# Random-feature attention: the third norm step of a chunk one slot earlier in a hand-written order

## The chip, the cores and the metric

The kernel runs on one core of one Trainium2 chip. The time is device microseconds of one execution of the whole program, from the first to the last instruction and the little around them. The program has sixteen layers in a row; the change lies in one of them.

## What is computed

The activation x has 4096 tokens of 128 channels (a batch of 16 by 256 tokens). The program adds sixteen sublayers to it in turn, each on a layer norm of x. The third one is a Performer block: attention with 16 heads of 8 channels by way of 32 random features, and a feed-forward behind it. The attention part of the reference, cut:

```python
def _phi(u, omega):
    proj = jnp.einsum('bhsk,mk->bhsm', u, omega)
    sq = 0.5 * jnp.sum(u * u, axis=-1, keepdims=True)
    stab = jnp.max(proj, axis=-1, keepdims=True)
    return jnp.exp(proj - sq - stab) / jnp.sqrt(m) + 1e-06
...
q = jnp.einsum('bsd,dhk->bhsk', x, wq)
...
pq = _phi(q * scale, omega)
pk = _phi(k * scale, omega)
kv = jnp.einsum('bhsm,bhsk->bhmk', pk, v)
z = jnp.sum(pk, axis=2)
num = jnp.einsum('bhsm,bhmk->bhsk', pq, kv)
den = jnp.einsum('bhsm,bhm->bhs', pq, z)
out = num / den[..., None]
```

The x that goes in here is the layer norm `(x - mean) / sqrt(var + 1e-5)` of the running x, without a gain. That norm is what the change touches.

## The kernel before, in words

Channels lie on the 128 partitions, tokens along the free axis. `self.x` is the running activation, `self.ha` its norm (both 128 x 4096), `self.hb` the attention's result. The work is cut in 8 chunks of 512 tokens (`CH`, `NCH`), 16 batch entries of 256 (`B`), and 32 tiles of 128 (`NTILE`). One batch entry is half a chunk.

`performer_attend` (line 2275) writes its order out by hand. Its list `steps` (2401 to 2406) has entries (slot, every, many, what). `tiles_in_slots` (2260) runs a counter k, here from -7 to 45. In each k it walks down the list, and where `(k - slot)` is a multiple of `every`, it calls `what` with the quotient. [...] So the list's order is the order within one k, and one chunk's work recurs every four k.

The steps that matter here, for chunk c with batch entries 2c and 2c + 1:

- `norm(0)`, `norm(1)`, `norm(2)` (2400): the three parts of the norm of x (`norm_x_step`, 1837; `norm_steps`, 1817). The first, `centre_step` (1759), is a matmul of x with the centring matrix, a copy from PSUM to `ha` on ACT, and a square `nsq` on POOL. The second, `spread_step` (1774), is a matmul of the square with a matrix of means, and a logarithm and an exponential on ACT that leave 1/sqrt(var) in `nrs`. The third, `scale` (1828), is one multiply on DVE, `ha <- ha * nrs` (128 x 512, by way of line 531).
- `project` (2287): two matmuls of `ha` with wq and wk (in the trace four records ps<-ha,w, as each fp32 matmul has two), copied on ACT to q and k (both named `q`), and squared on POOL.
- `values` (2306): four matmuls with `ha` as the stationary side (ps<-w,ha).
- `lengths` (2297): eight matmuls with 16 columns (ps<-w,sq), and on DVE a copy to `nrm` (2304).
- `features` (2315), per batch entry: sixteen small matmuls into four PSUM banks (ps<-w,q), and on DVE four maxima (2331), two small additions and four subtractions (f<-ps,sub).
- `raised` (2341): two exponentials on ACT, and a multiply-add on POOL (2345).
- `turn` (2363): four transposes of `f` (ps<-ct,f), copied on ACT to `ft`.
- `sums` (2347): eight matmuls with 33 columns (ps<-v,f), two multiplies on DVE to `kv`.
- `heads` (2372): matmuls ps<-ft,kv at 2377, `rd` on ACT, `ot` on DVE.
- `out` (2385): ps<-ot,w, and an addition on DVE into `hb`. `end(0)` to `end(2)` (2391): the norm of that result, with the same three parts, in place in `hb`.

PSUM has eight banks: four for the features (tag `f`), four for all else (tag `ps`), shared out by `share` (2407). Which of the four a matmul gets is decided when the program is built, by the place of the instructions that free them.

`norm_x_step` does nothing for a chunk whose norm the stage before has already made (`self.led`, 1839): `lead` (1862) does so for chunks 0 to NCH - 4 = 4. In this stage, then, the three norm steps run for chunks 5, 6 and 7 alone.

Of the kernel before, what the change touches and what calls it, by code (L numbers as in the profile page):

```python
# [21 lines left out]
NCH = NT // CH  # L22
# [469 lines left out]
class Net:  # L492
# [70 lines left out]
    def norm(self, src, dst, eps, g=None, b=None, rms=False, chunks=range(NCH)):  # L563

        nc = self.nc
        with ExitStack() as st:
            pool = self.pool(st, "norm", 2)
            pv = self.bank()
            last = len(chunks) - 1
            for n, c in enumerate(chunks):  # L570
                s, d = src[:, self.chunk(c)], dst[:, self.chunk(c)]
                sq = pool.tile([P, CH], F32, tag="sq", name="sq")
                if rms:
                    self.gt(sq, s, s, ALU.mult)
                else:
                    pc = self.bank()
                    self.mm(pc, self.k["cent"], s)
                    self.act(d, pc, AF.Copy)
                    self.gt(sq, d, d, ALU.mult)
                self.mm(pv[:8], self.k["vrow"][:, 7 - c : 15 - c], sq, start=n == 0, stop=n == last)  # L580
            rs = pool.tile([8, CH], F32, tag="rs", name="rs", bufs=1)
            self.act(rs, pv[:8], AF.Sqrt, bias=self.k[eps][:8])
            nc.vector.reciprocal(rs, rs)
            for c in chunks:
                s = src[:, self.chunk(c)] if rms else dst[:, self.chunk(c)]
                d = dst[:, self.chunk(c)]
                pb = self.bank()
                self.mm(pb, self.sel[:, c, :], rs)
                if g is None:
                    self.tt(d, s, pb, ALU.mult)  # L590
                else:
                    self.stt(d, s, g, pb, ALU.mult, ALU.mult)
                    if b is not None:
                        self.act(d, d, AF.Identity, bias=b)
# [1055 lines left out]
class Fast(Net):  # L1650
# [624 lines left out]
    def performer_attend(self, w):  # L2275
# [6 lines left out]
        with ExitStack() as st:  # L2282
# [108 lines left out]
            def end(i):  # L2391
# [8 lines left out]
            norm = lambda i: lambda c: self.norm_x_step(p, c, i)  # L2400
# [1 line left out]
                (13, 4, NCH, end(2)), (12, 4, NCH, end(1)), (11, 4, NCH, end(0)), (10, 4, NCH, out),  # L2402
                (7, 2, B, heads), (5, 2, B, sums), (3, 1, NTILE, turn), (1, 2, B, raised), (0, 2, B, features),
                (-1, 4, NCH, lengths), (-2, 4, NCH, values), (-3, 4, NCH, project),
                (-4, 4, NCH, norm(2)), (-6, 4, NCH, norm(1)), (-7, 4, NCH, norm(0)),
            ]
            with self.share(f=4, ps=4):
                self.tiles_in_slots(-7, NTILE + 14, steps)
# [1467 lines left out]
```

## Time and profile before

| | us |
|---|---|
| median of 3 runs (lowest, highest) | 4220.33 (4219.34, 4223.46) |
| profiled execution | 4218.15 |
| its span, first to last instruction | 4216.4 |
| attention part of the Performer block, about | 820 to 1015 |
| in it: TensorE busy | 170.78 of 195.00 |
| in it: DVE, ACT, POOL busy | 125.71, 97.47, 65.31 |

The profile is of one execution, on a machine of five engines: TensorE (PE, its weight loads PEld), VectorE (DVE), ScalarE (ACT), GpSimd (POOL) and SyncE (SP, which issues transfers). A row of a timeline has the start in us from the span's start, a length, the engine, the line in the kernel, the operation, what it writes and reads, a count where equal ones are merged, and in brackets how long the engine stood idle before it and whose end released it. Lines 504, 508, 528, 531, 534 and 543 are helpers that many steps call; the names of the tiles tell which step an instruction belongs to. The clock that is named with a stretch is the share of TensorE's full clock that was granted there.

### The profile page before, as it was taken

The numbers are of one execution on the slowest core, as the hardware profiler recorded it, in microseconds if no ns is written. First come the engines' busy times: TensorE is split into PE (matmuls) and PEld (weight loads), VectorE is DVE, ScalarE is ACT, GpSimd is POOL, SyncE is SP. The second block draws the span as 40 slices with busy tenths as digits, with TensorE's granted clock in tenths as the row PEclk, the third lists the DMA queues.
The fourth block names the chain that finished last, engine by engine and source line by source line (L and its number), as shares of the span: only waits on it lengthen the run. The fifth ranks groups of instructions, "written<-read, shape, count | busy, mean of one in ns | idle before, by whom it ended". The sixth has DMA issues, their size and how long they took to land. (4 is left out here: it accounts for less than half of the span.)

```text
span 4216.4 us, 74153 instructions
## 1 busy us (share of the span) xinstructions
PE 3831.5 (91%) x29030; PEld 2182.7 (52%) x29030; DVE 2551.0 (61%) x4503; ACT 2281.8 (54%) x4478; POOL 1853.7 (44%) x1632
## 2 busy tenths in 40 slices
PE   7999999998899999985989869888999999899978
PEld 3555466464455466454965459543444344455333
DVE  4776576374577477473346633556877676486474
ACT  6665466555766466652457634444554454774532
POOL 4754365232565166225433434454555455321251
PEclk8999999998999999996999979999999999999979
DMA  1800000000000000004920058100000000000000
GB/s 61 347 15 12 11 9 9 22 1 1 20 11 14 6 7 9 6 11 142 323 69 12 17 182 295 41 19 21 16 14 16 8 0 10 7 2 19 6 0 21
DMA packets 110086, 190.88 MB, mean 45 GB/s; under 512 B 16126, under 2 KB 70788, under 8 KB 109600
## 3 DMA queue, kind: packets, MB, share of 16 engines
q1 hardware_dynamic: 97248, 162.83, 11.7%
q0 software_dynamic: 9120, 18.51, 1.3%
q8 instruction: 231, 3.78, 0.4%
q10 hardware_dynamic: 3360, 4.72, 0.3%
q14 instruction: 127, 1.04, 0.1%
HBM read 118.28 MB, written 54.20 MB: 41 GB/s over the span
## 5 line engine op out<-in xcount | busy, mean ns | idle before, releaser
L528 ACT ACTIVATE pt<-ps 128x512 f32<-128x512 f32 x640 | 339.5, 600 | 337.5 <-PE ps L504 336.2
L504 PE MATMUL ps<-hb,w 128*128 128x512 f32 (+1 forms) x960 | 463.7, 617 | 3.9 <-issue 3.3
L504 PE MATMUL ps<-w,hb 128*128 128x512 f32 (+2 forms) x896 | 405.2, 573 | 27.3 <-DVE t L531 18.5
L534 POOL TENSOR_TENSOR t<-t,t 128x512 f32<-128x512 f32 x256 | 319.9, 1271 | 153.7 <-DVE t L531 107.8
L531 DVE TENSOR_TENSOR t<-ps,tab 128x512 f32<-128x512 f32 x512 | 317.5, 681 | 70.1 <-ACT sq L528 66.7
L534 POOL TENSOR_TENSOR t<-t,ss 128x1024 f32<-128x1024 f32 x128 | 243.7, 1904 | 195.2 <-ACT ss L528 194.0
L504 PEld LDWEIGHTS ps<-hb,w 128*128 128x128 f32 (+1 forms) x960 | 179.6, 191 | 261.8 <-issue 220.6
L528 ACT ACTIVATE qkt<-ps 128x512 f32<-128x512 f32 x256 | 140.6, 595 | 299.2 <-PE ps L508 299.2
L531 DVE TENSOR_TENSOR u<-u,ps 128x384 f32<-128x384 f32 (+1 forms) x206 | 121.8, 595 | 277.2 <-ACT u L528 114.9
L534 POOL TENSOR_TENSOR nsq<-ha 128x512 f32<-128x512 f32 x112 | 123.2, 1100 | 354.3 <-ACT ha L528 342.3
L531 DVE TENSOR_TENSOR ot<-ps,rd 128x512 f32<-128x512 f32 (+2 forms) x224 | 143.2, 639 | 209.8 <-ACT rd L528 209.8
L504 PEld LDWEIGHTS ps<-w,hb 128*128 128x128 f32 x896 | 154.1, 193 | 174.4 <-issue 111.7
L534 POOL TENSOR_TENSOR both<-pt 128x1024 f32<-128x1024 f32 x64 | 151.2, 2363 | 199.0 <-DVE pt L531 191.3
L504 PE MATMUL ps<-ot,w 128*128 128x512 f32 x448 | 213.6, 611 | 17.4 <-DVE ot L531 9.9
L504 PE MATMUL ps<-xt,w 128*128 128x128 f32 x1704 | 221.0, 280 | 1.6 <-ACT xt L528 1.5
L2225 POOL DMA_INDIRECT back<-y,x x142 | 139.1, 980 | 186.1 <-ACT y L528 69.5
L504 PE MATMUL ps<-u,w 128*128 128x512 f32 (+1 forms) x448 | 215.4, 605 | 3.4 <-POOL u L534 3.4
L504 PEld LDWEIGHTS ps<-xt,w 128*128 128x128 f32 x1704 | 204.5, 194 | 3.4 <-ACT xt L528 3.4
L528 ACT ACTIVATE u<-ps,w 128x512 f32<-128x512 f32 x160 | 107.7, 685 | 173.3 <-PE ps L504 170.6
L3479 PE MATMUL ps<-qkt 64*128 64x192 f32 (+1 forms) x2048 | 181.8, 311 | 9.6 <-ACT rd L528 9.6
L504 PE MATMUL ps<-ha,w 128*128 128x512 f32 x320 | 176.1, 672 | 11.6 <-ACT f L528 10.2
L504 PE MATMUL ps<-nsq,ct 128*128 128x512 f32 x272 | 154.5, 652 | 30.8 <-POOL nsq L534 26.6
(366 smaller groups left out, 8756.2 us busy)
## 6 DMA issues: line engine op xcount, KB each, us to landing
w<-in_moe_x SPq DMA_DIRECT2D x142, 533.0 KB
rows<-t SPq DMA_DIRECT2D x64, 520.0 KB
nrs<-nrow SPq DMA_DIRECT2D x220, 64.0 KB
x<-rows SPq DMA_DIRECT2D x142, 65.0 KB
w<-in_local_f SPq DMA_DIRECT2D x8, 659.5 KB
y<-back ACTq DMA_DIRECT2D x16, 256.0 KB
y<-back SPq DMA_DIRECT2D x16, 256.0 KB
w<-in_local_f SPq DMA_DIRECT2D x4, 658.5 KB
```

Of the source, the lines that this page charges most:

```text
L504: self.nc.tensor.matmul(out, lhsT, rhs, start=start, stop=stop)
L528: self.nc.scalar.activation(out, in_, func, **kw)
L531: self.nc.vector.tensor_tensor(out, a, b, op)
L534: self.nc.gpsimd.tensor_tensor(out, a, b, op)
L2225: nc.gpsimd.indirect_dma_start(views[i], bass.IndirectOffsetOnAxis(ap=x[:, C : C + 1].bitcast(I32), axis=0), y, None, bounds_check=2 * NT ...
L3479: nc.tensor.matmul(out, kt[rows, g, t * P : t * P + P], qt[rows, g, t * P : t * P + wide], start=(i, t) == (0, 0), stop=i == 1, skip_group ...
```

## The change

One number in the list of slots: `norm(2)` of chunk c runs at k = 4c - 5 in place of 4c - 4.

```diff
                 (-1, 4, NCH, lengths), (-2, 4, NCH, values), (-3, 4, NCH, project),
-                (-4, 4, NCH, norm(2)), (-6, 4, NCH, norm(1)), (-7, 4, NCH, norm(0)),
+                (-5, 4, NCH, norm(2)), (-6, 4, NCH, norm(1)), (-7, 4, NCH, norm(0)),
```

The slot 4c - 4 is even and holds `features` of a batch entry; the norm's entry stands behind it in the list. The slot 4c - 5 is odd and holds no features; in it the entry stands behind `end(0)`, `heads`, `sums`, `turn`, `raised` and `lengths`. On DVE the multiply `ha <- ha * nrs` of chunks 5, 6 and 7 thereby moves from the place behind the four subtractions of `features` to the place in front of its first maximum, right behind the copy of `nrm`. In the built program these three instructions are all that changes place, on any engine. Two things follow from it there: the projection waits for the multiply at its new place; and the banks of tag `ps` are dealt out otherwise from chunk 5 on. The centring matmul of the next chunk's `norm(0)`, which took the bank that `heads` had used and waited for `ot` on DVE, takes the bank of the first projection and waits for its copy q on ACT; the output matmul takes the bank of `heads`.

## The prediction

> **What bounds the kernel now.** Three views, in this order: the busy times of the page, to know which engine counts; the stretches of the stage, one for each group of four slots; and the timeline of two such groups side by side. TensorE is busy 91% of the span, so what it loses by standing still is what the stage can give.
>
> ```profile
> PE 3831.5 (91%) x29030; PEld 2182.7 (52%) x29030; DVE 2551.0 (61%) x4503; ACT 2281.8 (54%) x4478; POOL 1853.7 (44%) x1632
> ...
> 883.54:904.72 21.18, 19.07 (x184) 13.07 (x184) 15.46 (x31) 13.06 (x21) 8.49 (x9) 1.00 0.00 1
> 904.72:931.35 26.63, 23.24 (x184) 15.10 (x184) 16.77 (x32) 13.28 (x21) 8.72 (x9) 0.81 0.00 1
> 931.35:958.31 26.96, 23.57 (x185) 15.30 (x184) 16.77 (x32) 13.28 (x21) 8.70 (x9) 0.81 0.00 1
> 958.31:982.01 23.70, 20.31 (x180) 14.25 (x180) 16.05 (x32) 11.48 (x18) 7.67 (x8) 0.86 0.00 1
> ```
>
> The last four lines are stretches (start:end, length; busy time and count of PE, PEld, DVE, ACT, POOL; granted clock; DMA). Each starts where a group of four slots begins, with the transposes in front of a chunk's projection: chunks 4, 5, 6 and 7. Chunk 4's norm was made in the stage before (chunks up to NCH - 4 = 4 are led), those of 5, 6 and 7 are made here. Chunk 4's group has the 184 matmuls of chunk 5's, takes 21.18 us against 26.63, at a granted clock of 1.00 against 0.81. It is a specimen of the group without the multiply of `norm(2)` behind the features; the timeline shows what the difference consists of (start, length, engine, line, operation; in brackets the idle time before it and who ended it).
>
> ```profile
> 883.54 0.63 PE L508 MATMUL ps<-ct,f 128*128 128x128 f32 x4
> 884.01 1.98 PE L504 MATMUL ps<-ha,w 128*128 128x512 f32 x4
> 888.09 1.13 PE L504 MATMUL ps<-x,ct 128*128 128x512 f32 x2 [2.11 <-ACT q L528]
> 889.05 1.02 PE L504 MATMUL ps<-ot,w 128*128 128x512 f32 x2
> 890.44 1.17 PE L504 MATMUL ps<-w,q 32*128 32x128 f32 x32
> ...
> 899.46 2.17 POOL L2345 TENSOR_SCALAR f<-f 128x1024 f32<-128x1024 f32 x2 [2.90 <-ACT f L528]
> 899.52 0.29 DVE L2304 COPY nrm<-ps 128x128 f32<-128x128 f32 x1 [0.87 <-PE ps L504]
> 902.00 1.29 DVE L2331 TENSOR_REDUCE sub<-ps 128x16 f32<-128x512 f32 x2 [2.18 <-PE ps L504]
> 904.72 0.63 PE L508 MATMUL ps<-ct,f 128*128 128x128 f32 x4
> 906.36 1.29 DVE L531 TENSOR_TENSOR f<-ps,sub 128x512 f32<-128x512 f32 x2
> 907.57 1.03 DVE L531 TENSOR_TENSOR ha<-ha,nrs 128x512 f32<-128x512 f32 x1
> 907.68 1.06 ACT L528 ACTIVATE f<-f 128x1024 f32<-128x1024 f32 x1 [0.75 <-DVE f L531]
> 908.74 3.75 PE L504 MATMUL ps<-ha,w 128*128 128x512 f32 x4 [3.39 <-ACT f L528]
> ```
>
> Chunk 4's projection (ha,w) follows its transposes at once. Chunk 5's waits 3.39 us. The profile names ACT's exponential, which ended last (908.74); but the matmul reads `ha`, and the multiply that makes `ha` ended at 908.60, behind all of the features' work on DVE. So the wait that ends last here is the multiply's. Then the four projection matmuls take 3.75 us, not 1.98: TensorE runs at half clock. Looked at in pieces of 0.2 us the clock is 0.50 from 907.3 to 914.1, from 934.5 to 941.5 and from 961.9 to 965.3, each time out of such a gap.
>
> **The change, part by part.** Three DVE instructions move (chunks 5, 6, 7), nothing is added or removed; SP, POOL, ACT and PE keep their order. None of the three issues a DMA. At chunk 5 the multiply leaves its place behind the features (907.57) for the place behind the copy of `nrm` (899.81).
>
> Does it fit there? Its input `nrs` was finished by ACT at 894.95 (894.32 plus 0.63), and the square that reads the old `ha` on POOL at 891.95. DVE is idle from 899.81 to 902.00, when the features' matmuls end: 2.18 us of cover for a multiply of 1.03 us. It ends at about 900.84 and is free; without that cover it would hold up the first reduction by 1.03 us, three times. [...] The row of 1.03 us was taken beside a POOL operation; where POOL is still, the same multiply takes 0.68 (at 823.08). The new place is beside two POOL operations on `f`, 899.46 to 901.63. [...] By the row the multiply ends at 900.84. [...] What POOL loses to it is hidden, since the transposes that read these values come a slot or more later.
>
> **What is late next.** With `ha` there at 901 the projection starts behind its transposes, near 905.2. The next matmul is the centring of the following chunk (x,ct). In the changed program it takes the PSUM bank of the first projection, as it does at chunk 4, and so waits for ACT's copy q, which stands behind both exponentials; at chunk 4 that is the gap of 2.11 us. ACT's second exponential stays where it is (its features on DVE are not moved), so chunk 5 copies chunk 4: x,ct starts 4.55 us after the transposes start (888.09 - 883.54). The output matmul needs `ot`, which DVE has 1.03 us earlier than before.
>
> From the start of the transposes to the start of the next features' matmuls (w,q):
> - chunk 4: 890.44 - 883.54 = 6.90 us;
> - chunk 5: 915.45 - 904.72 = 10.73, saved 3.83;
> - chunk 6: 942.42 - 931.35 = 11.07, saved 4.17;
> - chunk 7: 966.99 - 958.31 = 8.68. No norm follows, so only `ot` gates the output. At chunk 4 `ot` ends 1.89 us after DVE leaves the features' last subtraction (886.38 to 888.27); here it leaves it at 961.16, so `ot` ends at 963.05, the output starts at some 963.15, and w,q 1.39 later, at 964.54: saved 2.45.
>
> Sum 10.45 us, of which the gaps give about 10.2 less what the waits for q and `ot` take back, and the lost half clock the rest.
>
> **The second slow window.** Chunks 5, 6 and 7 also lose 1.6 us each later in the group: from w,q to the group's end chunk 5 takes 15.90 us, chunk 6 15.89, chunk 4 14.28; chunk 7 15.02 against 13.42 (14.28 less the 0.86 of one spreading it hasn't). There the clock is 0.50 for one window of 3.4 us, and TensorE was not idle in front:
>
> ```profile
> 922.00:924.00 2.00, 2.00 (x20) 2.00 (x20) 1.66 (x5) 1.16 (x2) 0.00 (x0) 1.00 0.00 0
> 924.00:926.00 2.00, 2.00 (x7) 1.05 (x7) 0.29 (x1) 1.33 (x2) 1.45 (x2) 0.59 0.00 0
> 926.00:928.00 2.00, 2.00 (x21) 1.48 (x23) 0.00 (x0) 1.53 (x3) 0.64 (x1) 0.56 0.00 0
> ```
>
> [...] By the row, 4 us of narrow matmuls (33 and 16 columns, 920.36 to 924.3) are enough, where a counter window falls inside them. All drops here lie whole multiples of about 3.41 us apart. Such a stretch drops the clock in three groups of this stage and leaves it alone in three; chunk 5's, moved to 916.5 to 920.5, would leave 0.4 us of wide matmuls in the window that ends at 920.9, and with 0.36 us (948.3 to 951.7) the clock fell. So I count one of three windows gone, 1.61 us, and keep none and all for the range.
>
> **The sum.** 10.45 + 1.61 = 12.06 us off the profiled execution's 4218.15: 4206.1. The median of the runs shown is 2.18 higher, a shift that I keep: 4208.3. What follows the stage starts earlier by the same amount; the stage's only weight load lies in its first 20 us, so no transfer pins its end.
>
> **The rivals.**
> - Forecast, 0.78: 4208.3; own range 4203.5 (all three windows gone: 15.3 off the median is 4205.0, less 1.5 of scatter) to 4211.5 (none gone 4209.9, and the port rule's 0.9).
> - The clock doesn't follow, 0.09: the shorter gap of 2.1 us, with transposes and narrow matmuls in front, still halves it. For: narrow work alone did so at 924. Against: chunk 4 has just this sequence at 1.00. Price: one window of 1.61 in each group, 10.45 - 4.83 = 5.6 saved: 4214.7.
> - The multiply is not hidden, 0.06: POOL or the copy of `nrm` holds it, and the features start its 1.03 us later, three times: 10.45 - 3.09 = 7.4 saved, 4213.0. Against: the idle 2.18 us.
> - The gap was ACT's, 0.04: the projection really waits for the exponential that the profile names. Then nothing is saved, 4220.3. Against: chunk 4's projection ran 2.5 us before its exponential began.
> - Slower, 0.03: DVE works in order, so a multiply that waits for a late `nrs` holds the whole of the features behind it, then both exponentials, q, and the next centring. Place: between `nrm` and the first reduction. Price: each us that `nrs` comes after 900.97 (902.00 - 1.03). The saving of 3.48 us a group is eaten once `nrs` comes at 904.5; one slot later still, at 907.5, would give 4220.3 + 9 = 4229. Against: 894.95 in the row is 9.5 us ahead of that point.
>
> **How the numbers follow.** Two tenths of a per cent is about what a measurement of this kernel can tell from no change: 8.4 us. Faster by more needs 4211.9 or less: nearly all of the forecast and some of the third case, 0.76. Slower is the last rival, 0.03; the rest is 0.21. The range goes from the forecast's low end, 4203.5, up to 4214.5, and leaves the clock's rival at its edge and the two last ones out.
>
> **What would show it.** In the changed profile: no idle time in front of ha,w at chunks 5 to 7; about 2.1 us in front of x,ct, ended by q; ha,w at 2.0 us for its four; the multiply between the copy of `nrm` and the reduction, whose idle time shrinks from 2.18 to about 1.1; groups of 21.2 to 22.8 us, near clock 1.00. It is wrong if ha,w still waits, if the reductions start late, or if the clock stays near 0.81.

## The result, and the profile after

The changed kernel takes 4214.95 us (median of 20 runs, 4202.33 to 4222.73) against 4221.45 us for the kernel before, timed on the same chip (20 runs, 4217.73 to 4229.9). The ratio is 0.9978, with a 95% interval from 0.997 to 0.9985: some 9 us less. (It is taken over all runs of both; the two medians lie 6.5 us apart, the two means 8.7.) The two kernels were paired twice more, on two chips: 0.9976 (0.9967 to 0.9986), 10.1 us, and 0.9974 (0.9965 to 0.9983), 10.9 us. The change makes the kernel faster by about a quarter of a per cent, near ten microseconds. The profiled execution, the fastest of the twenty, took 4202.33 us and its span 4200.5.

First the busy times of the page, then the stretches of the stage as they were shown of before (start:end, length; busy time and count of PE, PEld, DVE, ACT, POOL; granted clock; DMA): the groups of chunks 4, 5, 6 and 7.

```profile
PE 3809.4 (91%) x29030; PEld 2173.6 (52%) x29030; DVE 2554.9 (61%) x4503; ACT 2284.6 (54%) x4478; POOL 1853.7 (44%) x1632
...
884.53:905.91 21.38, 19.33 (x184) 12.99 (x184) 17.59 (x31) 13.08 (x21) 8.69 (x9) 1.00 0.00 1
905.91:927.03 21.12, 19.07 (x184) 13.08 (x184) 16.76 (x32) 13.08 (x21) 8.86 (x9) 1.00 0.00 1
927.03:948.16 21.13, 19.08 (x184) 13.08 (x184) 16.77 (x32) 13.08 (x21) 8.87 (x9) 1.00 0.01 2
948.16:971.14 22.98, 20.55 (x180) 14.27 (x180) 14.74 (x31) 11.28 (x18) 7.55 (x8) 0.85 0.00 1
```

Chunks 5 and 6 have become what chunk 4 was: 21.12 and 21.13 us at a clock of 1.00, where they took 26.63 and 26.96 at 0.81. Chunk 7 gained little, 23.70 to 22.98, and its clock is still 0.85. TensorE's busy time fell by 22.1 us over the span with the same 29030 matmuls: a matmul at half clock is counted busy for about twice as long (four of the projection 3.75 us for 1.98), so most of such a fall is clock and not work. Only 8.4 us of it lies in these three groups (67.12 to 58.70); the rest is clock elsewhere in this one execution, and no effect of the change is shown there. The timeline of one group shows how it comes about (start, length, engine, line, operation; in brackets the idle time and who ended it).

```profile
900.65 2.49 POOL L2345 TENSOR_SCALAR f<-f 128x1024 f32<-128x1024 f32 x2 [2.90 <-ACT f L528]
900.72 0.29 DVE L2304 COPY nrm<-ps 128x128 f32<-128x128 f32 x1 [0.87 <-PE ps L504]
900.93 1.31 DVE L531 TENSOR_TENSOR ha<-ha,nrs 128x512 f32<-128x512 f32 x1
902.00 1.17 PE L504 MATMUL ps<-w,q 32*128 32x128 f32 x32
903.19 1.29 DVE L2331 TENSOR_REDUCE sub<-ps 128x16 f32<-128x512 f32 x2 [0.95 <-PE ps L504]
905.91 0.63 PE L508 MATMUL ps<-ct,f 128*128 128x128 f32 x4
```

The multiply now stands at 900.93 and ends at 902.24; DVE then still waits 0.95 us for the features' matmuls. Their first maximum starts 1.19 us after the matmuls themselves (902.00 to 903.19), 2.54 us after POOL's first operation, exactly as before (899.46 to 902.00): the multiply cost nothing. The same stretch on TensorE alone:

```profile
905.91 0.63 PE L508 MATMUL ps<-ct,f 128*128 128x128 f32 x4
906.38 1.98 PE L504 MATMUL ps<-ha,w 128*128 128x512 f32 x4
910.40 1.13 PE L504 MATMUL ps<-x,ct 128*128 128x512 f32 x2 [2.04 <-ACT q L528]
911.37 1.02 PE L504 MATMUL ps<-ot,w 128*128 128x512 f32 x2
912.23 0.60 PE L508 MATMUL ps<-ct,f 128*128 128x128 f32 x4
912.76 1.17 PE L504 MATMUL ps<-w,q 32*128 32x128 f32 x32
```

The projection has no idle time in front of it any more. The idle 3.39 us have become 2.04 us in front of the next chunk's centring (x,ct), ended by ACT's q, and the four projection matmuls take 1.98 us for 3.75. From the transposes to the next features (w,q) chunk 5 takes 6.85 us for 10.73. Below, "front part" is this length, and "rest" is that from w,q to the next group's transposes.

The profiled execution is 15.8 us shorter than that of before (4218.15 to 4202.33), more than the change gives. The groups of chunks 5 to 7 account for 12.06 of it (77.29 to 65.23). Of what remains, 3.1 us lie before the stage, 1.1 in its last slots and 3.9 behind it, and in the stage's earlier groups 4.1 us run the other way, at a granted clock of 0.85 for 0.91. None of these places holds a moved instruction. That is why the timed ratio, and not the difference of two profiles, says what the change is worth.

### The profile page after: what moved, and what is told of

Read it like the earlier page. It is cut to its first block, busy times and chain, and to the rows that moved or that the text cites. A ratio compares the mean times of both kernels' runs of the same rounds, so it can differ in the third digit from the quotient of the medians.

```text
span 4200.5 us, 74148 instructions
## 1 busy us (share of the span) xinstructions
PE 3809.4 (91%) x29030; PEld 2173.6 (52%) x29030; DVE 2554.9 (61%) x4503; ACT 2284.6 (54%) x4478; POOL 1853.7 (44%) x1632
## 3 DMA queue, kind: packets, MB, share of 16 engines
q14 instruction: 127, 1.04, 0.1%
## 5 line engine op out<-in xcount | busy, mean ns | idle before, releaser
L531 DVE TENSOR_TENSOR pt<-ps,w 128x384 f32<-128x384 f32 (+1 forms) x320 | 170.8, 576 | 16.1 <-PE ps L504 12.9
```

The source lines that it names most:

```text
L531: self.nc.vector.tensor_tensor(out, a, b, op)
```

## The experiments

The theory: the multiply held the projection up; at its new place it is hidden; what is left is the wait for q; and a good part of the gain is the clock, which fell only because the gap was long. The main rivals: the gap was ACT's; the clock plays no part, or falls all the same; the multiply is only just hidden, and a later `nrs` would turn the gain into a loss.

| kernel | us | ratio to before | interval | groups of chunks 5, 6, 7 |
|---|---|---|---|---|
| before_again | 4220.25 | 0.9999 | 0.9989 to 1.0009 | 26.37, 26.84, 23.64 |
| after_again | 4210.64 | 0.9976 | 0.9967 to 0.9986 | 22.75, 21.12, 22.92 |
| fill_the_gap | 4216.85 | 0.9988 | 0.9981 to 0.9995 | 24.36, 24.41, 21.03 |
| between_the_halves | 4217.67 | 0.9988 | 0.9982 to 0.9995 | 23.40, 21.80, 24.91 |
| nrs_late | 4177.15 | 0.9988 | 0.9981 to 0.9994 | 26.03, 21.14, 22.91 |
| fill_after | 4171.47 | 0.997 | 0.9959 to 0.9982 | 21.12, 21.12, 19.76 |
| ot_first | 4170.9 | 0.9966 | 0.9953 to 0.9978 | 21.22, 21.22, 18.79 |
| ot_and_q_first | 4163.25 | 0.9952 | 0.9939 to 0.9964 | 20.96, 20.96, 18.79 |
| after_third | 4170.58 | 0.9974 | 0.9965 to 0.9983 | 22.74, 21.12, 22.91 |
| four_multiplies | 4182.93 | 0.9998 | 0.999 to 1.0006 | 24.73, 26.08, 22.98 |
| own_norm_behind_ot | 4167.26 | 0.996 | 0.9946 to 0.9974 | 20.66, 20.66, 18.16 |
| own_norm_behind_ot_q_first | 4157.62 | 0.9941 | 0.9927 to 0.9954 | 20.39, 20.40, 19.86 |

The first four ran on one chip beside a before of 4220.68 us, the next four on another (4181.22), the last four on a third (4182.74). Only ratios are compared across these three sets.

### The two kernels once more

**after_again** is the changed kernel and **before_again** the kernel before, unedited.

> The changed kernel again, for a second profile at another position of the clock's counter. Measure: A, from the transposes in front of a chunk's projection to the next features' matmuls (w,q), and B, from there to the next transposes in front of a projection. In the first profile A was 6.85, 6.85, 7.11 us and B 14.27, 14.28, 15.87 for chunks 5, 6, 7 (before: A 10.73, 11.07, 8.68, B 15.90, 15.89, 15.02). Theory (place of the multiply): A stays at 6.8 to 7.2 for chunks 5 and 6 in every execution, since no idle gap near 3.4 us is left; only B, and A of chunk 7, move by about 1.6 us where a counter window falls on narrow matmuls. Rival (the shorter gap halves the clock in most executions, and the first profile was a lucky one): A is 8 us or more at chunk 5 or 6, ha,w or x,ct at half clock. Rival (the banks that are dealt otherwise cost later): the part from 1002 us on is longer than before's by some us.

> The kernel before again, with a profile at another position of the counter. Theory: A stays near 10.7 to 11.1 at chunks 5 and 6 in every execution, because the idle stretch of 3.4 us and the narrow work in front of it always hold a whole counter window; B is 14.3 or 15.9, by the window. Rival (A is also a matter of luck): A falls to 9 us or less at a chunk, with ha,w at 1.98 us.

In before_again the gap is again 3.39 us at each of the three chunks. At chunk 5 the profile puts it down to ACT's exponential, at 6 and 7 to the multiply; chunk 6 on TensorE:

```profile
937.13 3.75 PE L504 MATMUL ps<-ha,w 128*128 128x512 f32 x4 [3.39 <-DVE ha L531]
```

The same wait, with the name that the matmul's operands call for. In after_again chunk 6 repeats (front part 6.84), but chunk 5's takes 8.08 us. TensorE there:

```profile
910.35 0.63 PE L508 MATMUL ps<-ct,f 128*128 128x128 f32 x4
910.82 1.98 PE L504 MATMUL ps<-ha,w 128*128 128x512 f32 x4
914.84 1.13 PE L504 MATMUL ps<-x,ct 128*128 128x512 f32 x2 [2.05 <-ACT q L528]
915.81 1.84 PE L504 MATMUL ps<-ot,w 128*128 128x512 f32 x2
917.44 1.06 PE L508 MATMUL ps<-ct,f 128*128 128x128 f32 x4
```

The gap is the same 2.05 us and x,ct runs at full clock, but from 915.8 on the output's matmuls take 1.84 us for 1.02: the clock fell. So the gap that is left is long enough for that in some executions, here at a price of 1.2 us in the front part and 0.4 behind it. The expectation had the front parts of chunks 5 and 6 at 6.8 to 7.2 us in every execution; at chunk 5 its rival came true. Its other rival, that the banks dealt otherwise cost time later, did not: from the matmul ps<-ot,w with 2.15 us of idle time in front to the end, before took 3204.2 and 3200.8 us, the changed kernel 3198.3 and 3199.7. **after_third**, the changed kernel on the third chip, shows the same lengths, with 8.02 at chunk 5.

> The changed kernel a third time, on the same chip as the next three, as their base. Theory: A is 6.8 to 7.0 us at chunks 5 and 6, or about 8.1 where a counter window ends on the gap in front of x,ct; its ratio to before is 0.997 to 0.999 as in the two earlier sets.

### How much of the gain is clock

**fill_the_gap** keeps the multiply where it was before, and puts three extra matmuls into the bank that the projection then overwrites; their results are not used.

```diff
                     pq = self.bank()
+                    if side == 0 and c not in self.led:
+                        for _ in range(3):
+                            self.mm(pq, w["wo"], self.x[:, s])
                     self.mm(pq, w[wn], h0[:, s])
```

> The kernel before, with three matmuls whose result is overwritten put in front of the projection of chunks 5, 6, 7: TensorE works through some 2.6 us of the 3.4 it waits for the multiply, and the multiply stays behind the features. It parts the gap from the half clock that follows it. Theory (more than half of the gain is the clock's): ha,w starts when it did, but takes 1.98 us in place of 3.75, and x,ct and ot,w run at full clock: A is about 8.4 at chunks 5 and 6 and 7.5 at chunk 7 (worked out from before's rows: 10.73 - 2.35, 11.07 - 2.68, 8.68 - 1.15), some 6 us saved of the 10.45. Rival (the gap itself is the gain, the slow clock is hidden behind q and ot anyway): A stays at 10 us or more, nothing saved.

Chunk 5's front part on TensorE:

```profile
907.38 0.63 PE L508 MATMUL ps<-ct,f 128*128 128x128 f32 x4
907.85 2.74 PE L504 MATMUL ps<-x,w 128*128 128x512 f32 x6
911.31 1.98 PE L504 MATMUL ps<-ha,w 128*128 128x512 f32 x4 [0.73 <-DVE ha L531]
913.49 1.12 PE L504 MATMUL ps<-x,ct 128*128 128x512 f32 x2 [0.19 <-DVE ot L531]
```

The projection still waits for `ha`, as late after the transposes as before (3.93 us against 4.02). But the clock stays up, and the front part is 8.46 us for 10.73 and 11.07 at chunks 5 and 6. Of the 3.88 us that the change takes from chunk 5's front part in the first profile (10.73 to 6.85), 2.27 come back by keeping TensorE busy with useless work, and only 1.61 are the lateness of the multiply itself. The rest of these groups is unchanged (15.90 and 15.95 us): their second fall of the clock doesn't need this gap. At chunk 7 it was absent (rest 13.43 for 15.02). By the timed ratio, 0.9988, useless work gives about 5 us.

**fill_after** does the same in the changed kernel, with two extra matmuls between the halves of the projection, their results again unused.

```diff
+                    if side == 1 and c not in self.led:
+                        for _ in range(2):
+                            self.mm(pq, w["wo"], self.x[:, s])
```

> The changed kernel with two matmuls whose result is overwritten in front of the second projection of chunks 5, 6, 7: the gap of 2.05 us in front of x,ct is worked through to some 0.3. Theory (the gap that the change leaves halves the clock in some executions, as at chunk 5 of the second profile and chunk 7 of the first, and costs 0.3 to 1.2 us where it does): A is 6.85 to 7.0 at chunks 5 and 6 and about 6.2 at chunk 7, the time 0 to 2 us below the changed kernel's. Rival (the second copy q, now later, becomes the bound of the transposes behind): A is 7.3 or more.

Chunk 6 on TensorE:

```profile
940.50 1.02 PE L504 MATMUL ps<-ha,w 128*128 128x512 f32 x2
941.85 1.12 PE L504 MATMUL ps<-x,ct 128*128 128x512 f32 x2 [0.33 <-ACT q L528]
```

x,ct waits for q only 0.33 us and starts as late as ever, 4.49 us after the transposes (937.36): q is what gates it. None of the three groups loses clock. Chunk 4's, whose gap of 2.12 us was not filled, does in the same profile: its front part takes 7.82 us for 6.92. Chunk 7, which kept a gap of 2.43 us in all three profiles of the changed kernel, takes 19.76 us for 22.9: all that it failed to gain was clock. By its time (0.997) the kernel can't be told apart from the change.

### Is the multiply hidden, and with how much to spare?

**between_the_halves** puts the multiply between the two halves of the features' work on DVE, later than the change does and earlier than before.

```diff
                 for k in range(2):
+                    if k == 1 and b % 2 == 0 and c + 1 < NCH:
+                        norm(2)(c + 1)
...
-                (-5, 4, NCH, norm(2)), (-6, 4, NCH, norm(1)), (-7, 4, NCH, norm(0)),
+                (-6, 4, NCH, norm(1)), (-7, 4, NCH, norm(0)),
```

> The multiply of chunks 5, 6, 7 stands between the two halves of the features on DVE: behind two of the four subtractions, in front of the last two maxima. Theory (what ends last after the change is the features' second exponential and the copy q behind it, so that any DVE time spent in front of it is paid in full): the projection waits some 0.6 us at most, the second half starts 0.7 to 1.0 us later, and A is 7.5 to 7.9 us at chunks 5 and 6, about 1 us more than with the multiply in front of the features, and 3 less than before. Rival (only the end of the multiply matters, not what it delays): A is 6.9. Rival (the gap was ACT's): A is 10.7 or more, as before.

Chunk 6, all engines but the weight loads, with lines left out:

```profile
939.64 0.68 DVE L531 TENSOR_TENSOR ha<-ha,nrs 128x512 f32<-128x512 f32 x1
940.24 1.28 DVE L2333 TENSOR_REDUCE sub<-ps 128x16 f32<-128x512 f32 x2
940.47 1.95 PE L504 MATMUL ps<-ha,w 128*128 128x512 f32 x4 [0.30 <-DVE ha L531]
...
944.70 1.12 PE L504 MATMUL ps<-x,ct 128*128 128x512 f32 x2 [2.28 <-ACT q L528]
```

Here the multiply is not covered: it holds the second half of the features up by its 0.68 us, and ACT's q and the centring come later by the same. The front part is 7.52 us against 6.84. That is still far less than behind the features (11.07 in before), and the projection starts at 940.47, ahead of both exponentials on ACT (940.69 and 943.10). By time (0.9988) about half of the change's gain is left; two of the three groups lost clock in this profile. With POOL still, the multiply takes 0.68 us; in the change it takes 1.31, beside POOL.

**nrs_late** takes the changed kernel and makes the second norm step one slot later, directly in front of the multiply: meant as the slower rival's case.

```diff
-                (-5, 4, NCH, norm(2)), (-6, 4, NCH, norm(1)), (-7, 4, NCH, norm(0)),
+                (-5, 4, NCH, norm(1)), (-5, 4, NCH, norm(2)), (-7, 4, NCH, norm(0)),
```

> The changed kernel with norm(1) of chunks 5, 6, 7 one slot later too, so that nrs is made on ACT behind the two exponentials and reaches DVE after the multiply's turn has come. This is the slower rival of the prediction, brought about. Theory (the multiply at the head of the features holds all behind it, each us in full): the multiply waits for nrs, the first maximum starts 0.7 to 1.5 us later than with nrs early, x,ct as much later, and A is 7.5 to 8.4 us at chunks 5 and 6 where the clock is full, still some 2.5 under before: saved in all 5 to 8 us. Rival (the 2.2 us of DVE idle in front of the features still cover it): A stays at 6.85.

Chunk 5, all engines but the weight loads, with lines left out:

```profile
905.64 0.63 ACT L528 ACTIVATE nrs<-nrs 128x512 f32<-128x512 f32 x1
906.11 1.17 PE L504 MATMUL ps<-w,q 32*128 32x128 f32 x32
...
906.37 0.69 DVE L531 TENSOR_TENSOR ha<-ha,nrs 128x512 f32<-128x512 f32 x1 [2.12 <-ACT nrs L528]
...
907.30 1.29 DVE L2331 TENSOR_REDUCE sub<-ps 128x16 f32<-128x512 f32 x2 [0.23 <-PE ps L504]
```

The multiply does wait 2.12 us for `nrs`, with the features behind it. But `nrs` is ready at 906.27, 0.16 us after w,q starts, and the multiply, with POOL still, takes 0.69 us: it ends at 907.06, before the features' matmuls let the first maximum start. That maximum stands 1.19 us after w,q, as in the changed kernel, and waits for PE, not for the multiply. Nor is w,q put off: it follows the w,q before it by 10.37 us, as in after_again. So one slot is not late enough, and this run does not test the rival's price. Chunk 6's front part is 6.86 us. The expected loss of a microsecond a group did not come. In the profile the only loss lies in chunk 5's group, where the clock was halved from 915.5 to 919 and again from 925.8 to 932.5; the timed interval (0.9981 to 0.9994) overlaps the change's, so whether the kernel gives anything back is not settled.

**four_multiplies** makes the multiply truly late: three more of its size stand in front of it, their results unused.

```diff
+                    if i == 2 and c not in self.led:
+                        spare = p.tile([P, CH], F32, tag="spare", name="spare", bufs=1)
+                        for _ in range(3):
+                            self.tt(spare, self.ha[:, self.chunk(c)], self.ha[:, self.chunk(c)], ALU.mult)
                     self.norm_x_step(p, c, i)
```

> The changed kernel with three multiplies more (128x512, result not used) in front of the moved one at chunks 5, 6, 7: the price of work at that place once the idle time of DVE is used up. The moved multiply of 1.31 us leaves 0.95 us of idle in front of the first maximum; three more take 2.1 us where POOL is still and up to 3.9 beside it. Theory (each us behind the cover is paid in full): the first maximum starts 1.1 to 2.6 us later against w,q, the gap in front of x,ct grows by the same, and A grows by the same, to 8.0 to 9.5 us; a gap that grows over 3 us also halves the clock, which adds to A. Rival (x,ct has slack, or something else ends the wait): A stays at 6.85.

Chunk 5, first DVE, then TensorE:

```profile
910.30 3.48 DVE L531 TENSOR_TENSOR spare<-ha 128x512 f32<-128x512 f32 x3
913.88 0.69 DVE L531 TENSOR_TENSOR ha<-ha,nrs 128x512 f32<-128x512 f32 x1
914.49 1.28 DVE L2331 TENSOR_REDUCE sub<-ps 128x16 f32<-128x512 f32 x2
```

```profile
911.38 1.17 PE L504 MATMUL ps<-w,q 32*128 32x128 f32 x32
...
915.76 1.98 PE L504 MATMUL ps<-ha,w 128*128 128x512 f32 x4
921.70 1.76 PE L504 MATMUL ps<-x,ct 128*128 128x512 f32 x2 [3.96 <-ACT q L528]
```

The first maximum starts 3.11 us after w,q in place of 1.19: 1.92 us late. The gap in front of x,ct is longer by just that (2.04 to 3.96), and the clock falls behind it in both groups. Chunk 5 takes 24.73 us and chunk 6 26.08, against 22.74 and 21.12 in after_third. The whole gain is gone (0.9998): what isn't covered at this place is paid for in full, and with clock on top. This is the run that tests the slower rival's price, and it bears it out.

### A better order

The gap that is left is made by q, which stands behind the exponentials on ACT. Four orders of the list try to bring it, and `ot`, forward. **ot_first** lists `heads` and `sums` in front of the attention's own norm (`end`) and `out`.

```diff
-                (13, 4, NCH, end(2)), (12, 4, NCH, end(1)), (11, 4, NCH, end(0)), (10, 4, NCH, out),
-                (7, 2, B, heads), (5, 2, B, sums), (3, 1, NTILE, turn), (1, 2, B, raised), (0, 2, B, features),
+                (7, 2, B, heads), (5, 2, B, sums), (13, 4, NCH, end(2)), (12, 4, NCH, end(1)), (11, 4, NCH, end(0)), (10, 4, NCH, out),
+                (3, 1, NTILE, turn), (1, 2, B, raised), (0, 2, B, features),
```

> The changed kernel with heads and sums listed in front of end(2), end(1), end(0): on DVE ot and kv stand directly behind the features, in front of the two operations of the attention's own norm; the banks are dealt so that x,ct waits for ot and not for q. Theory (the group is bound by DVE's features and what is behind them): ot is 1.6 us earlier, x,ct starts 1.2 us earlier, A is 5.6 to 5.9 us at chunks 4, 5, 6: 5 to 7 us below the changed kernel. Rival (q on ACT remains the wait): A stays at 6.85.

**ot_and_q_first** also lists `project` between `turn` and `raised`, so that ACT copies q before the exponentials.

> As the one before, and project is listed in front of raised: on ACT the two copies q stand in front of the exponentials, and x,ct waits for a copy that is early. Theory: x,ct follows the projection with under 0.5 us of idle, the output matmul waits for ot alone, A is 4.6 to 5.0 us at chunks 4, 5, 6: 8 to 12 us below the changed kernel. The exponentials are about 1 us later, which their readers, a slot and more behind, do not feel. Rival (the later exponentials are felt: POOL's multiply-add and the transposes behind it come late): B grows by 0.5 us or more over 14.28.

The front parts come out near what was expected: 5.60 us at chunks 5 and 6 in the first, 4.81 in the second. But the rest gives most of it back, 15.62 and 16.15 us for 14.28. TensorE now waits for POOL's square of the norm of x (nsq, 0.51 and 1.05 us), and 0.25 us for the attention's own norm (hb), which stands behind the heads. So only the last part of the latter, the one that stands on DVE in front of `ot`, was moved: **own_norm_behind_ot** lists `end(2)` alone behind `sums`, and **own_norm_behind_ot_q_first** also lists `project` between `turn` and `raised`.

```diff
-                (13, 4, NCH, end(2)), (12, 4, NCH, end(1)), (11, 4, NCH, end(0)), (10, 4, NCH, out),
-                (7, 2, B, heads), (5, 2, B, sums), (3, 1, NTILE, turn), (1, 2, B, raised), (0, 2, B, features),
-                (-1, 4, NCH, lengths), (-2, 4, NCH, values), (-3, 4, NCH, project),
+                (12, 4, NCH, end(1)), (11, 4, NCH, end(0)), (10, 4, NCH, out),
+                (7, 2, B, heads), (5, 2, B, sums), (13, 4, NCH, end(2)), (3, 1, NTILE, turn), (-3, 4, NCH, project), (1, 2, B, raised), (0, 2, B, features),
+                (-1, 4, NCH, lengths), (-2, 4, NCH, values),
```

> Only end(2), the last step of the attention's own norm, is listed behind heads and sums; end(0) and end(1) stay in front of them, so the order on TensorE, ACT and POOL is the changed kernel's. In the two kernels before in which heads and sums were moved in front of all three, A fell to 5.6 and 4.8 us but B rose from 14.28 to 15.6 and 16.2. Theory (B rose because end(0) came later, and with it the square on POOL and its matmul): here A is 5.6 to 5.8 at chunks 4 to 6 and B stays at 14.28: a group of 19.9 to 20.1, some 1.2 us less a chunk, 6 to 8 us below the changed kernel in all. Rival (a group is bound at about 21 us by another loop, so that what A gives B takes back): A 5.6, B 15.4 or more.

> As the one before, and project in front of raised, so that the copies q on ACT do not wait behind the exponentials. Theory: A 4.8 and B 14.3 at chunks 4 to 6, a group of 19.1, 2 us less a chunk than the changed kernel, 10 us or more in all. Rival (a loop of about 21 us binds): A 4.8, B 16 or more, no better than the one before.

Both expected the rest to stay near 14.28 us. It does not: 15.06 at chunk 6 in the first, 15.59 in the second, between the theory and its rival. The wait for hb is gone, the one for POOL's square is not (0.51 and 1.05 us); the remainder was not followed up.

The last one on TensorE, chunk 5:

```profile
915.52 1.98 PE L504 MATMUL ps<-ha,w 128*128 128x512 f32 x4
917.33 1.02 PE L504 MATMUL ps<-x,ct 128*128 128x512 f32 x2
918.39 1.10 PE L504 MATMUL ps<-ot,w 128*128 128x512 f32 x2
...
923.16 1.12 PE L504 MATMUL ps<-nsq,ct 128*128 128x512 f32 x2 [1.04 <-POOL v L2312]
924.12 1.02 PE L504 MATMUL ps<-hb,ct 128*128 128x512 f32 x2
```

The gap in front of x,ct is gone; 1.04 us of it is back in front of the spreading (nsq,ct), whose square POOL now reaches later (it ends at 923.11; the profile names the short fill of `v` behind it). The front part is 4.81 us, the rest 15.58. Two of the four, ot_and_q_first (0.9952) and own_norm_behind_ot_q_first (0.9941, 0.9927 to 0.9954), beat both kernels; the latter has the lowest ratio of all, with 25 us less than before, more than twice the change's gain. Its profile, of the slowest of its five runs (4167.02 us), shows only part of this: the three groups are 6.1 us shorter than in after_third (66.77 to 60.65). The order acts on the other chunks too; where the rest lies was not followed up.

## Why the prediction was right, and where it was off

Forecast were 4208.3 us, 12.06 less than before, with a range from 4203.5 to 4214.5. The ratio puts the change at 4211.0 on the median that the forecast started from, 9.3 us less: inside the range. The median itself, 4214.95, stands just above it, beside a median of before that is 1.1 us higher.

- **The wait that ended last was the multiply's**: shown. With the multiply moved the projection starts behind its transposes, and before_again names `ha` itself at two of three chunks. The rival that had the gap down to ACT falls: in between_the_halves the projection starts on the multiply's end, ahead of both exponentials.
- **The multiply fits into DVE's idle time**: shown, with 0.95 us to spare, where "about 1.1" was expected. Its length was mis-sized: 1.31 us against 1.03. Counted from POOL's first operation it ends after 1.59 us; the row gave 1.38 (899.46 to 900.84), so it was too cheap. POOL's two operations took 2.49 us for 2.17: side by side, both took longer. No run shows the term of 0.9 us in the forecast's own range: the multiply ended at 902.24, and the first maximum started 2.54 us after POOL's first operation in both profiles. (The 0.68 us that the prediction read at 823.08 are not quite beside a still POOL, which starts at 823.24; between_the_halves shows the same length with POOL idle.)
- **What is late next** was right in each part: x,ct waits for q, starts 4.49 us after the transposes (4.55 predicted), and the gap is 2.04 (2.1). The front part is 6.85 at chunk 5 for 6.90.
- **Chunk 7's 2.45 us** is the term that failed. `ot` came when it should (the output starts 4.88 us after the transposes, 4.84 predicted), but the sum then took full clock for granted. A gap of 2.43 us stood in front of the output in every profile of the change, and the clock fell behind it each time; in four_multiplies, where it lay across two windows (below), it did not, and the front part took 6.34 us. The whole group gave 0.72 us (23.70 to 22.98); fill_after shows what it gives with the clock held, 19.76.
- **The second slow window, 1.61 us**, was mis-sized. The sum carried the place of the windows over from the one profile of before, and they stand elsewhere in each execution (below), so that one in three was a guess and not a working. Of three, those of chunks 5 and 6 were gone in the first profile (the rest 14.27 and 14.28 for 15.90 and 15.89), two and not one. But in two of three profiles chunk 5 lost 1.2 us of front part to a fall of the clock that was given only 0.09 as a rival, and chunk 7 kept its loss. The first profile's sum over the three groups is 12.06 us, the predicted number, by terms that cancel: 5.51 + 5.83 + 0.72. The repeat on the first set's chip gives 3.62 + 5.72 + 0.72 = 10.06. The timed pairs give 9.3, 10.1 and 10.9 us: the sum without the window term, 10.45, was nearer than the one with it. No profile of the changed kernel shows the 15.3 us at the range's low end, with all three windows gone: chunk 7's rest took 15.87, 16.34 and 16.39 us, against 13.42 in fill_after, where its clock stayed up.
- **The slower rival's price**, a microsecond for each one that the features start late, is borne out by four_multiplies (1.92 us late, 1.92 more of gap, and clock on top). That a slot later would bring `nrs` so late is not: in nrs_late it came 0.16 us after w,q, which in the profile of before is 900.97, the very point from which the prediction began to count.

**When the clock falls.** The traces say more on this than the prediction had. In each of the fourteen profiles the granted clock is 1.00 or 0.50, and any two of its changes lie a whole multiple of 3.413 us apart. A window is here one step of this grid; where the prediction and the expectations speak of a counter, the spacing is all that the traces show. Where the windows begin differs from one execution to the next, from 0.16 to 3.27 us after the first instruction. Here are the windows around the gap of chunk 5, two of the first profile of the change and then two of after_again (start:end, length; busy times; granted clock; DMA):

```profile
905.87:909.29 3.42, 2.49 (x10) 1.00 (x9) 3.35 (x7) 2.02 (x3) 1.05 (x1) 1.00 0.00 0
909.29:912.70 3.41, 2.29 (x8) 1.18 (x8) 1.99 (x6) 2.15 (x4) 2.67 (x3) 1.00 0.00 0
...
912.47:915.88 3.41, 1.36 (x4) 0.56 (x4) 2.97 (x7) 2.12 (x4) 2.46 (x3) 1.00 0.00 0
915.88:919.30 3.42, 3.42 (x23) 1.95 (x25) 0.69 (x1) 1.19 (x2) 2.96 (x4) 0.50 0.00 0
```

In the first profile the end of a window cuts the gap of 2.04 us in two, and the clock stays. In the second the same gap lies whole in one window, TensorE is busy 1.36 us of 3.41 in it, and the next window runs at half clock. All fourteen profiles have 26 gaps of 1.9 to 2.5 us between 880 and 972 us. The 15 that have 1.83 us or less in one window left the clock alone; the 11 that have 2.05 us or more halved it. None of these gaps fills a window: 2.05 us of 3.41 were enough.

The second slow window fits as well, if a narrow matmul counts for little. In the profile of before TensorE is busy without a break from 920.95 to 924.36, and the next window is slow. An estimate: let a matmul record of 512 columns on 128 x 128 of the array count 0.43 us (two take 1.02, one 0.59), and a smaller one less in proportion to its columns and its share of the array. Then this window is used 28%. Of the 336 windows at full clock between 880 and 972 us, the 37 used 37.7% or less by this estimate were each followed by half clock, the 299 used 38.4% or more were not. Over the whole spans the two kinds overlap between 31% and 44%. This is read from the traces; no run was built to test it.

## What to carry to other kernels

When the operand of a waiting matmul is made by another engine, look at what that engine does in front of it: here a multiply of 1.31 us, moved into an idle stretch of 2.18 us, cost nothing, as the stretch's end didn't move. Price an idle gap of the matmul engine with the matmuls behind it too: here the gap itself was the smaller half, and filling it with useless work won back 2.3 of 3.9 us. A gap that is left is a risk by how much of it can fall into one window of 3.41 us (here 2.05 us or more halved the clock behind it, 1.83 us or less did not); as the windows stood elsewhere in each execution, one profile doesn't settle it. After such a move look for what is late next, as it is likely cheaper to move two or three neighbours together than one alone.

## What the runs showed of the hardware

A gap of 2.05 us was followed by half of TensorE's clock in some executions and not in others of the same program, by its place in the windows of 3.41 us: chunk 5 took 6.85 us of front part in one profile and 8.08 and 8.02 in two. Beside POOL's two multiply-adds VectorE's multiply took 1.31 us, for 0.68 with POOL still (between_the_halves), and POOL's two took 2.49 us for 2.17. And the three chips differ by more than the change is worth: the kernel before takes 4220.68, 4181.22 and 4182.74 us on them. In the profiles all of that lies behind this stage, from the first matmul behind the attention part to the end: 3192.6 us in the first profile of the changed kernel, 3151.9 in after_third. The ratios were therefore taken beside runs of before on the same chip.
